# Order of turns, copies and projections in the fourth and the last four attention units

## The chip, the cores and the metric

The kernel runs on one core of a Trainium2 chip, as one launch. The metric is device time in microseconds (us); a run's time is that of the whole program on the core. The profiled execution has a span, from its first to its last instruction, and a time of its own, which is a little longer than the span.

## The reference

The input x has 32 batches of 100 tokens of width 512, the context has 722 tokens per batch. The reference computes x + attention(layernorm(x), context) and then x + feed-forward(layernorm(x)). The attention has 16 heads of width 32; its mask is lower triangular over 100 queries and 722 keys, so only the first 100 context tokens of a batch ever count:

```python
q = (Q @ WQ.T).reshape(B, Sq, NHEAD, D_K).transpose(0, 2, 1, 3)
k = (K @ WK.T).reshape(B, Skv, NHEAD, D_K).transpose(0, 2, 1, 3)
v = (V @ WV.T).reshape(B, Skv, NHEAD, D_K).transpose(0, 2, 1, 3)
scores = jnp.einsum('bhqd,bhkd->bhqk', q, k) / jnp.sqrt(jnp.float32(D_K))
causal = jnp.tril(jnp.ones((Sq, Skv), dtype=bool))
attn = jax.nn.softmax(jnp.where(causal, scores, -jnp.inf), axis=-1)
y = jnp.einsum('bhqk,bhkd->bhqd', attn, v).transpose(0, 2, 1, 3).reshape(B, Sq, D_MODEL)
return y @ Wfc.T + bfc
```

The feed-forward part has a shared expert for all 3200 tokens and 16 experts; each expert takes the 12 tokens of each batch with the highest routing score, and each is gelu(x Wg) * (x Wu) times Wd. All is float32.

## The kernel before

**Arithmetic.** A float32 matmul is made of three products: both operands are split into a rounded high part and the low remainder (a cast on ScalarE, a subtraction on VectorE or GpSimd), and high*high, high*low and low*high are added in PSUM (`mm3`, line 49, matmuls at line 56).

**Units.** Attention runs over 32 units. Unit u is block sb = u // 4 (four batches, 400 tokens) and column group c = u % 4 (four heads, 128 columns). `cur` holds the tiles by unit. The steps of a unit, each a small function:

- `kload(u)` (SyncE DMA of k from DRAM, tile kt), `qproj(u)` and `qkeep(u)`: q into PSUM (pool `a_kv`, two buffers) and its copy on ScalarE;
- `scores(u)`: 16 matmuls into the one buffer of tile sc;
- `sm_max(u, hb)` on VectorE, `sm_sub(u, hb)` on GpSimd, `sm_exp(u, hb)` on ScalarE, `sm_sum(u, hb)` on VectorE and `sm_mul(u, hb)` on GpSimd: softmax in two halves, hb = 0 and 1;
- `p_turn(u, b)`, `turns`: transposes of the probabilities of batch b of the block (0 to 3) into PSUM tile ms (pool `a_ms`, two buffers); `p_keep(u, b)`, `keeps`: the copies to tile pt on ScalarE. With two buffers the turns of batches 2 and 3 wait for the copies of 0 and 1, and `values` for the copy of 2;
- `values(u)`: attention times v into an ms tile; `y_keep(u)`: split of the result and its store to DRAM (yD).

The units overlap: the loop's pass u does q of unit u, the softmax of unit u - 1 and the turns and values of unit u - 2. The loop also projects k and v for later blocks: `kproj` (into a_kv), `kkeep` (copy kk on ScalarE and a store kD on SyncE), `vproj`, `vkeep`, and `vload(sb)`, which loads a block's v (tile v, 100 partitions, 800 KB) for its four units. Passes with no v left to project put `scores(u)` at their end (`ahead`).

**The order.** It is written out by hand: under `manual_schedule` TensorE, ScalarE, VectorE, SyncE and GpSimd each work their instructions strictly in program order. Who is ready later holds up what stands behind it on the same engine, and the DMAs of SyncE are issued in that order too.

**The last four units.** Pass 28 (`u == NU - 4`) is the last of the loop. Passes 29, 30 and 31 stand in `last_units(pr)`, where work of the feed-forward part is mixed in. `pr` prepares the first 384 tokens (three row tiles of 128): `pr.load_y()` loads attention output (yh, yl) back from yD, right after the loop and so ahead of pass 29 on SyncE; `pr.fc(i)` multiplies row tile i by Wfc into a_kv; `pr.add`, `pr.bias`, `pr.stats`, `pr.rsqrt`, `pr.norm` make the residual and the layer norm; `pr.turn(i)` transposes the row tile on TensorE and splits it (xh on ScalarE, xl on VectorE). `F.chunk_load`, `F.chunk_cast` and `F.chunk_low` bring and split the first weights of the feed-forward part. `F.preps[1]` is the same preparation for the next group of tokens. From `F.begin` on (gate_up of chunk 0) the feed-forward matmuls run.

Of the kernel before, what the change touches and what calls it, by code (L numbers as in the profile page):

```python
# [60 lines left out]
def attention(tc, K, F):  # L61
    nc = tc.nc
    with ExitStack() as ctx, ExitStack() as kvctx:
# [57 lines left out]
        def split_wc(w, c, r, eng=None):  # L121
            cs = slice(c * 128, (c + 1) * 128)
            split(WH[w][:, :, cs], WL[w][:, :, cs], r.rearrange("p (d n) -> p d n", d=NC4), eng)
# [122 lines left out]
        def qproj(u):  # L246
            sb, c = divmod(u, NC4)
            cs = slice(c * 128, (c + 1) * 128)
            nh, nl = cur["xh", sb], cur["xl", sb]
            pq = ps_kv.tile([128, D], F32, name="kv")  # L250
            mm3(nc, pq[:, 0:SB], [((WH[2][:, d, cs], WL[2][:, d, cs]),
                                   (nh[:, d, :], nl[:, d, :])) for d in range(NC4)])
            return pq

        def qkeep(u, pq):
            q = qp.tile([128, SB], F32, name="q")
            nc.scalar.copy(q, pq[:, 0:SB])
            cur["q", u] = q

        def scores(u):  # L260
            q, kt = cur["q", u], cur["k", u]
            sc = ps_sc.tile([S, 4, D], F32, name="sc")
            for b in range(4):
                cs = slice(b * S, (b + 1) * S)
                for h in range(4):
                    rows = slice(32 * h, 32 * h + 32)
                    nc.tensor.matmul(sc[:, h, cs], q[rows, cs], kt[rows, cs], start=True, stop=True)  # L267
            cur["sc", u] = sc
# [20 lines left out]
        def sm_exp(u, hb):  # L289
            p = cur["p", u, hb][0]  # L290
            for bb in range(2):
                b = u // NC4 * 4 + hb * 2 + bb
                nc.scalar.activation(p[:, bb], p[:, bb], AF.Exp, scale=rstd[:, b:b + 1])  # L293
# [8 lines left out]
        def sm_mul(u, hb):  # L302
            pv, sm = cur["p", u, hb][1], cur["sm", u, hb]
            nc.gpsimd.tensor_tensor(pv, pv, sm[:, :, None].to_broadcast([S, 8, S]), ALU.mult)  # L304
# [8 lines left out]
        def p_keep(u, b):  # L313
            pt = ptp.tile([128, 4, S], F32, name="pt")[0:S]
            nc.scalar.copy(pt, cur["tp", u, b][0:S, :, 0:S])  # L315
            cur["pt", u, b] = pt
# [20 lines left out]
        NU = nsb * NC4  # L337
# [78 lines left out]
        def turns(u, *bs):  # L416
            for b in bs:
                p_turn(u, b)

        def keeps(u, *bs):  # L420
            for b in bs:
                p_keep(u, b)
# [8 lines left out]
        def last_units(pr):  # L431

            gp, mt = nc.gpsimd, pr.pt

            def kt_bank():
                return ps_kv.tile([128, D], F32, name="kv").rearrange("p (c t) -> p c t", c=NC4)

            def maxes(u):
                for hb in range(2):
                    sm_max(u, hb)  # L440
                    sm_sub(u, hb)

            u = NU - 3
            kload(u)
            for i in range(pr.nt):
                pr.load_x(i)
            kload(u + 1)
            sm_max(u - 1, 0)
            sm_sub(u - 1, 0)
            y_keep(u - 3)  # L450
            sm_max(u - 1, 1)
            sm_sub(u - 1, 1)
            qkeep(u, qproj(u))
            turns(u - 2, 0, 1)
            keeps(u - 2, 0, 1)
            turns(u - 2, 2, 3)
            sm_exp(u - 1, 0)
            keeps(u - 2, 2, 3)
            sm_exp(u - 1, 1)
            for hb in range(2):  # L460
                sm_sum(u - 1, hb)
                sm_mul(u - 1, hb)
            pr.fc(0)
            F.chunk_load()
            values(u - 2)

            u = NU - 2
            scores(u - 1)
            y_keep(u - 3)
            pr.add(0)  # L470
            pr.bias(0)
            maxes(u - 1)
            pr.bias(1)
            pr.stats(0)
            pr.rsqrt(0)
            qkeep(u, qproj(u))
            turns(u - 2, 0, 1)
            keeps(u - 2, 0, 1)
            sm_exp(u - 1, 0)
            sm_exp(u - 1, 1)  # L480
            pr.fc(1)
            pr.norm(0)
            for hb in range(2):
                sm_sum(u - 1, hb)
                sm_mul(u - 1, hb)
            turns(u - 2, 2, 3)
            keeps(u - 2, 2, 3)
            pr.add(1)
            kload(u + 1)
            F.chunk_load()  # L490
            pr.store(0)
            pr.bias(2)
            values(u - 2)

            u = NU - 1
            scores(u - 1)
            y_keep(u - 3)
            maxes(u - 1)
            pr.fc(2)
            pr.add(2)  # L500
            pr.stats(1)
            pr.rsqrt(1)
            pr.stats(2)
            pr.rsqrt(2)
            F.ask(1, lambda: ps_kv.tile([128, D], F32, name="kv"))
            F.preps[1].load_x(0)
            F.preps[1].load_x(1)
            turns(u - 2, 0, 1)
            keeps(u - 2, 0, 1)
            qkeep(u, qproj(u))  # L510
            pr.pt = kt_bank
            pr.turn(0)
            pr.pt = mt
            pr.norm(1)
            pr.store(1)
            turns(u - 2, 2, 3)
            keeps(u - 2, 2, 3)
            pr.norm(2)
            pr.store(2)
            sm_exp(u - 1, 0)  # L520
            values(u - 2)
            sm_sum(u - 1, 0)
            sm_mul(u - 1, 0)
            y_keep(u - 2)
            pr.turn(1)
            sm_exp(u - 1, 1)
            sm_sum(u - 1, 1)
            sm_mul(u - 1, 1)
            F.chunk_cast(0, 0)

            scores(u)
            F.chunk_low(0, 0, gp)
            F.preps[1].fc(0)
            maxes(u)
            turns(u - 1, 0, 1)
            keeps(u - 1, 0, 1)
            turns(u - 1, 2, 3)
            keeps(u - 1, 2, 3)
            F.preps[1].fc(1)
            F.chunk_cast(0, 1)  # L540
            sm_exp(u, 0)
            sm_sum(u, 0)
            sm_mul(u, 0)
            pr.turn(2)
            sm_exp(u, 1)
            F.chunk_low(0, 1, gp)
            values(u - 1)
            sm_sum(u, 1)
            sm_mul(u, 1)
            y_keep(u - 1)  # L550
            F.chunk_cast(0, 2)
            scctx.close()
            F.open_gu()
            F.begin(pr.done())
            F.chunk_low(0, 2, gp)
            F.preps[1].add(0)
            F.preps[1].add(1)
            for i in range(3):
                F.chunk_cast(1, i)
                F.chunk_low(1, i, gp)  # L560
            F.preps[1].bias(0)
            F.preps[1].bias(1)
            turns(u, 0, 1)
            keeps(u, 0, 1)
            pr.logits()
            turns(u, 2, 3)
            keeps(u, 2, 3)
            F.begun()
            values(u)
            pr.tokens()  # L570
            y_keep(u)

        with tc.manual_schedule(engines={mybir.EngineType.Pool}):
            wq = prologue()
            ahead = False
            for u in range(NU - 3):
                sb, c = divmod(u, NC4)
                a, back = u - 1, u - 2
                a = a if a >= 0 else None
                back = back if back >= 0 else None  # L580
# [50 lines left out]
                if u == 1:  # L631
# [1 line left out]
                    wq_keep(2, wq[2])  # L633
                    sm_sum(a, 0)
                    sm_mul(a, 0)
                if a is not None and u > 2:
                    sm_exp(a, 0)
                if back is not None:
                    p_turn(back, 0)
                    p_turn(back, 1)  # L640
                    p_keep(back, 0)
                    p_keep(back, 1)
                if u == 2:
                    p_turn(back, 2)
                    p_turn(back, 3)
                    p_keep(back, 2)
                    p_keep(back, 3)
                    split_wc(2, 3, wq[3])
                    xt_split(1, 0)
                    sm_exp(a, 0)  # L650
                if xn:
                    x_stats(*xn)
                    if xn[1] == 3:
                        x_rstd(xn[0])
                if a is not None and u > 1:
                    sm_exp(a, 1)
                    sm_sum(a, 0)
                    sm_mul(a, 0)
                pk = kproj(j, ck) if kv else None
                if kv and vv:  # L660
                    kkeep(j, ck, pk)
                if u == 1:
# [2 lines left out]
                    sm_mul(a, 1)  # L665
                if c == 1 and u > 1 or u == NU - 4:
                    vload(sb)
                if back is not None and u > 2:
                    p_turn(back, 2)
                    p_turn(back, 3)  # L670
                    p_keep(back, 2)
                    p_keep(back, 3)
                if u == 1:
                    vkeep(j, ck, vproj(j, ck))
                    wq_less(3, wq[3])
                if kv and not vv:
                    kkeep(j, ck, pk)
                if a is not None and u > 1:
                    sm_sum(a, 1)
# [733 lines left out]
```

## Time and profile before

| | us |
|---|---|
| median of 3 runs | 1656.32 |
| lowest and highest run | 1654.76, 1657.05 |
| the profiled execution's own time | 1656.77 |
| its span | 1655.0 |
| TensorE (PE) busy in it | 1642.3 |
| VectorE (DVE) busy | 913.1 |
| ScalarE (ACT) busy | 697.4 |
| GpSimd (POOL) busy | 623.9 |

The page gives the time at which each engine was busy and the chain of waits that ended last. In the timelines a row is: start in us, length in us, engine, line, operation, output<-inputs, shape, count; in brackets the idle time of the engine just before the row, and what ended it. PEld is TensorE's loading of weights. SPq is SyncE's queue: a row there is the issue of a DMA, not its transfer. Attention lies in the first 360 us of the span (pass 3 starts near 55 us, pass 28 near 303, pass 31 near 330), and the feed-forward part fills the rest.

### The profile page before, as it was taken

The numbers are of one execution on the slowest core, as the hardware profiler recorded it, in microseconds if no ns is written. First come the engines' busy times: TensorE is split into PE (matmuls) and PEld (weight loads), VectorE is DVE, ScalarE is ACT, GpSimd is POOL, SyncE is SP. The second block draws the span as 40 slices with busy tenths as digits, with TensorE's granted clock in tenths as the row PEclk, the third lists the DMA queues.
The fourth block names the chain that finished last, engine by engine and source line by source line (L and its number), as shares of the span: only waits on it lengthen the run. The fifth ranks groups of instructions, "written<-read, shape, count | busy, mean of one in ns | idle before, by whom it ended". The sixth has DMA issues, their size and how long they took to land.

```text
span 1655.0 us, 27948 instructions
## 1 busy us (share of the span) xinstructions
PE 1642.3 (99%) x10722; PEld 1506.0 (91%) x10722; DVE 913.1 (55%) x2178; ACT 697.4 (42%) x1152; POOL 623.9 (38%) x501
## 2 busy tenths in 40 slices
PE   9999999999999999999999999999999999999999
PEld 8888888889899998999999999999999999999998
DVE  6878777665433434344655555555555555555542
ACT  4666666553111211123444444444444444444442
POOL 2778777660111011010743334433344443344001
PEclk9999999999999999999999999999999999999999
DMA  8566665645231223211545555455555455555452
GB/s 258 169 198 200 202 195 173 211 153 185 90 108 49 88 88 111 81 62 30 191 161 159 150 164 170 144 162 150 159 169 161 148 152 161 162 163 160 138 160 62
DMA packets 113493, 243.81 MB, mean 147 GB/s; under 512 B 16609, under 2 KB 64834, under 8 KB 113360
## 3 DMA queue, kind: packets, MB, share of 16 engines
q1 hardware_dynamic: 99856, 216.34, 39.8%
q0 software_dynamic: 13088, 25.22, 8.0%
q8 instruction: 84, 1.38, 0.3%
q14 instruction: 49, 0.40, 0.1%
q10 hardware_dynamic: 416, 0.48, 0.1%
HBM read 188.25 MB, written 53.73 MB: 146 GB/s over the span
## 4 chain that ended last, share of the span: by engine, by line
PE 95%; DVE 1%; POOL 1%; DMA 1%; ACT 1%; issue 1%; SPq 0%; POOLq 0%; ACTq 0%
PE gu L56 49%; PE dn L56 25%; PE kv L56 11%; PE m L56 3%; PE ms L310 2%; PE ms L325 1%; PE sc L267 1%; POOL p L287 1%; DMA yD<-y 0%; DVE p L278 0%; DMA yh<-yD 0%; PE m L1194 0%; DMA raw<-wA 0%; ACT pt L315 0%; POOL p L304 0%
## 5 line engine op out<-in xcount | busy, mean ns | idle before, releaser
L56 PE MATMUL gu<-xh,whl 128*128 128x384 f32 (+1 forms) x3200 | 641.2, 332 | 0.0
L56 PEld LDWEIGHTS gu<-xh,whl 128*128 128x128 f32 x3200 | 555.8, 188 | 20.3 <-issue 1.2
L1018 POOL DMA_INDIRECT gx<-xnD,iq x192 | 245.2, 1277 | 395.6 <-DVE big L1061 296.3
L56 PE MATMUL dn<-whl,hh 128*128 128x512 f32 x1168 | 366.3, 395 | 0.0
L821 DVE TENSOR_TENSOR whl<-wraw,whl 128x1536 fp32r<-128x1536 f32 x142 | 249.7, 1759 | 197.8 <-ACT whl L820 178.6
L56 PE MATMUL gu<-xl,whl 128*128 128x384 f32 (+1 forms) x1600 | 335.9, 331 | 0.0
L56 PEld LDWEIGHTS gu<-xl,whl 128*128 128x128 f32 x1600 | 279.1, 188 | 0.2 <-DVE xl L1052 0.2
L855 ACT CAST hh<-g 128x384 fp32r<-128x384 f32 (+1 forms) x200 | 101.0, 505 | 409.8 <-DVE g L852 379.2
L56 PEld LDWEIGHTS dn<-whl,hh 128*128 128x128 f32 x1168 | 215.7, 188 | 35.7
L852 DVE TENSOR_TENSOR g<-g,gu 128x384 f32<-128x384 f32 (+1 forms) x200 | 108.3, 541 | 251.0 <-PE gu L56 245.1
L820 ACT CAST whl<-wraw 128x1536 fp32r<-128x1536 f32 x142 | 209.8, 1477 | 57.2 <-PE dn L56 53.4
L56 PE MATMUL dn<-whl,hl 128*128 128x512 f32 x584 | 230.5, 395 | 0.0
L851 ACT ACTIVATE g<-gu 128x384 f32<-128x384 f32 (+1 forms) x200 | 96.2, 481 | 229.4 <-PE gu L56 229.4
L856 DVE TENSOR_TENSOR hl<-g,hh 128x384 fp32r<-128x384 f32 (+1 forms) x200 | 111.8, 559 | 114.3 <-ACT hh L855 113.8
L1073 POOL DMA_INDIRECT out_dram<-x,isl x48 | 77.7, 1619 | 171.0 <-ACT x L1072 161.2
L56 PEld LDWEIGHTS dn<-whl,hl 128*128 128x128 f32 x584 | 109.5, 188 | 26.1
L287 POOL TENSOR_TENSOR p<-p,mx 100x800 f32<-100x800 f32 x64 | 103.7, 1636 | 35.9 <-DVE mx L278 33.3
L304 POOL TENSOR_TENSOR p<-p,sm 100x800 f32<-100x800 f32 x64 | 97.4, 1528 | 35.6 <-DVE sm L299 26.2
L278 DVE CUSTOM_DVE_ANT_0 p<-sc,mask 100x100 f32<-100x100 f32 x512 | 95.5, 255 | 0.5 <-PE sc L267 0.5
L1110 POOL TENSOR_TENSOR x<-x,bfc 128x512 f32<-128x512 f32 x23 | 30.4, 1345 | 155.6 <-DMA x<-x 154.0
L293 ACT ACTIVATE p<-p,rstd 100x400 f32<-100x400 f32 x128 | 73.6, 624 | 17.6 <-POOL p L287 16.9
L1062 ACT CAST xh<-big 128x512 fp32r<-128x512 f32 x59 | 36.6, 621 | 101.4 <-DVE big L1061 101.4
(158 smaller groups left out, 1581.2 us busy)
## 6 DMA issues: line engine op xcount, KB each, us to landing
wraw<-wE SPq DMA_DIRECT2D x144, 768.0 KB
yD<-y SPq DMA_DIRECT2D x31, 400.0 KB
xr<-xT SPq DMA_DIRECT2D x32, 200.0 KB
vD<-vt SPq DMA_DIRECT2D x25, 256.0 KB
v<-vD SPq DMA_DIRECT2D x8, 800.0 KB
xnD<-xn SPq DMA_DIRECT2D x25, 256.0 KB
out_dram<-x SPq DMA_DIRECT2D x25, 256.0 KB
kt<-kD SPq DMA_DIRECT2D x31, 200.0 KB
```

The lines of the kernel that those rows point to most:

```text
L56: r = nc.tensor.matmul(out, t[0][a], t[1][b], start=(first and i == 0), stop=(last and i == n - 1))
L278: nc.vector.tensor_tensor_reduce(out=p[:, bb, h, :], in0=sc[:, h, cs], in1=mask, scale=ISCALE, scalar=NEG, op0=ALU.add, op1=ALU.max, accum ...
L287: nc.gpsimd.tensor_tensor(pv, pv, mx[:, :, None].to_broadcast([S, 8, S]), ALU.subtract)
L304: nc.gpsimd.tensor_tensor(pv, pv, sm[:, :, None].to_broadcast([S, 8, S]), ALU.mult)
L820: nc.scalar.copy(h, r)
L821: nc.vector.tensor_tensor(l, r, f32(h), ALU.subtract)
L851: nc.scalar.activation(g[:, 0:t], pg[:, 0:t], AF.Gelu)
L852: nc.vector.tensor_tensor(g[:, 0:t], g[:, 0:t], pu[:, 0:t], ALU.mult)
L855: nc.scalar.copy(hh[:, 0:t], g[:, 0:t])
L856: nc.vector.tensor_tensor(hl[:, 0:t], g[:, 0:t], f32(hh[:, 0:t]), ALU.subtract)
L1018: nc.gpsimd.indirect_dma_start(out=g[:, k, :], out_offset=None, in_=self.K.xn.rearrange("t (a f) -> (t a) f", f=128), in_offset=bass.Indir ...
L1073: ins = nc.gpsimd.indirect_dma_start(out=self.K.out, out_offset=bass.IndirectOffsetOnAxis(ap=r.isl[:, i:i + 1], axis=0), in_=o, in_offset= ...
```

## The change

The change moves calls; it adds and removes none, and every instruction keeps its operands.

- Pass 3: the turns and copies of batches 2 and 3 go right behind those of 0 and 1, ahead of the exponentials and of `kproj`, as pass 2 already had them (`early`).
- Pass 28: `kproj` is called ahead of the turns of batches 2 and 3 (as TensorE had it already); the copies of batches 2 and 3 and `kkeep`, with its DMA, go ahead of the second half's exponential, and so ahead of `vload`.
- Pass 29: `pr.fc(0)` and the first half's exponential go between the two pairs of turns.
- Pass 30: the turns and copies of batches 2 and 3 go ahead of the second half's exponential and of `pr.norm(0)`, behind `pr.fc(1)`.
- Pass 31: the turns and copies of batches 2 and 3 go ahead of `pr.turn(0)`; `scores(u)` and the second half's exponential, sum and product go ahead of `pr.turn(1)`.

```diff
--- before.py
+++ after.py
@@ -453,14 +453,14 @@
             qkeep(u, qproj(u))
             turns(u - 2, 0, 1)
             keeps(u - 2, 0, 1)
+            pr.fc(0)
+            sm_exp(u - 1, 0)
             turns(u - 2, 2, 3)
-            sm_exp(u - 1, 0)
             keeps(u - 2, 2, 3)
             sm_exp(u - 1, 1)
             for hb in range(2):
                 sm_sum(u - 1, hb)
                 sm_mul(u - 1, hb)
-            pr.fc(0)
             F.chunk_load()
             values(u - 2)
 
@@ -477,14 +477,14 @@
             turns(u - 2, 0, 1)
             keeps(u - 2, 0, 1)
             sm_exp(u - 1, 0)
+            pr.fc(1)
+            turns(u - 2, 2, 3)
+            keeps(u - 2, 2, 3)
             sm_exp(u - 1, 1)
-            pr.fc(1)
             pr.norm(0)
             for hb in range(2):
                 sm_sum(u - 1, hb)
                 sm_mul(u - 1, hb)
-            turns(u - 2, 2, 3)
-            keeps(u - 2, 2, 3)
             pr.add(1)
             kload(u + 1)
             F.chunk_load()
@@ -508,13 +508,13 @@
             turns(u - 2, 0, 1)
             keeps(u - 2, 0, 1)
             qkeep(u, qproj(u))
+            turns(u - 2, 2, 3)
+            keeps(u - 2, 2, 3)
             pr.pt = kt_bank
             pr.turn(0)
             pr.pt = mt
             pr.norm(1)
             pr.store(1)
-            turns(u - 2, 2, 3)
-            keeps(u - 2, 2, 3)
             pr.norm(2)
             pr.store(2)
             sm_exp(u - 1, 0)
@@ -522,13 +522,13 @@
             sm_sum(u - 1, 0)
             sm_mul(u - 1, 0)
             y_keep(u - 2)
-            pr.turn(1)
+            scores(u)
             sm_exp(u - 1, 1)
             sm_sum(u - 1, 1)
             sm_mul(u - 1, 1)
+            pr.turn(1)
             F.chunk_cast(0, 0)
 
-            scores(u)
             F.chunk_low(0, 0, gp)
             F.preps[1].fc(0)
             maxes(u)
@@ -633,30 +633,42 @@
                     wq_keep(2, wq[2])
                     sm_sum(a, 0)
                     sm_mul(a, 0)
-                if a is not None and u > 2:
+                if a is not None and u > 3:
                     sm_exp(a, 0)
                 if back is not None:
                     p_turn(back, 0)
                     p_turn(back, 1)
                     p_keep(back, 0)
                     p_keep(back, 1)
-                if u == 2:
+                early = u in (2, 3)
+                if early:
                     p_turn(back, 2)
                     p_turn(back, 3)
                     p_keep(back, 2)
                     p_keep(back, 3)
+                if u == 2:
                     split_wc(2, 3, wq[3])
                     xt_split(1, 0)
+                if early:
                     sm_exp(a, 0)
                 if xn:
                     x_stats(*xn)
                     if xn[1] == 3:
                         x_rstd(xn[0])
+                pk = None
+                if u == NU - 4:
+                    pk = kproj(j, ck)
+                    p_turn(back, 2)
+                    p_turn(back, 3)
+                    p_keep(back, 2)
+                    p_keep(back, 3)
+                    kkeep(j, ck, pk)
                 if a is not None and u > 1:
                     sm_exp(a, 1)
                     sm_sum(a, 0)
                     sm_mul(a, 0)
-                pk = kproj(j, ck) if kv else None
+                if kv and not pk:
+                    pk = kproj(j, ck)
                 if kv and vv:
                     kkeep(j, ck, pk)
                 if u == 1:
@@ -665,7 +677,7 @@
                     sm_mul(a, 1)
                 if c == 1 and u > 1 or u == NU - 4:
                     vload(sb)
-                if back is not None and u > 2:
+                if back is not None and not early and u < NU - 4:
                     p_turn(back, 2)
                     p_turn(back, 3)
                     p_keep(back, 2)
@@ -673,7 +685,7 @@
                 if u == 1:
                     vkeep(j, ck, vproj(j, ck))
                     wq_less(3, wq[3])
-                if kv and not vv:
+                if kv and not vv and u < NU - 4:
                     kkeep(j, ck, pk)
                 if a is not None and u > 1:
                     sm_sum(a, 1)
```

## The prediction

> **What bounds the kernel now.** I read the page first (shares, then the chain), then TensorE's waits by stretch, then the timelines of the engines and of SP's queue around the edited units, then DMA by stretch.
>
> ```profile
> PE 1642.3 (99%) x10722; PEld 1506.0 (91%) x10722; DVE 913.1 (55%) x2178; ACT 697.4 (42%) x1152; POOL 623.9 (38%) x501
> PE 95%; DVE 1%; POOL 1%; DMA 1%; ACT 1%; issue 1%; SPq 0%; POOLq 0%; ACTq 0%
> ```
>
> TensorE is busy 1642.3 of 1655.0 us and carries 95% of the chain. The edit removes no matmul, so it can only gain out of 12.7 us of TensorE idle, and any new TensorE wait is added whole. TensorE's waits in the window from 300 us (the last units lie at 303 to 360):
>
> ```profile
> PE ms L325 <- ACT pt L315: 1.5, 3, 0.8
> PE kv L56 <- DMA yh<-yD: 0.8, 1, 0.8
> PE ms L310 <- POOL p L304: 0.6, 1, 0.6
> PE ms L1050 <- DVE xn L1140: 0.5, 1, 0.5
> PE ms L310 <- ACT pt L315: 0.4, 1, 0.4
> ```
>
> With 0.2 for x L1119 that is 4.0 us; unit 3 has one more wait, 1.83 us at 63.23. So about 5.9 us is the most to be had. Where they sit in unit 29, TensorE's timeline:
>
> ```profile
> 313.52 0.85 PE L310 MATMUL ms<-ident,p 100*100 100x100 f32 x8
> 314.75 0.86 PE L310 MATMUL ms<-ident,p 100*100 100x100 f32 x8 [0.39 <-ACT pt L315]
> 316.43 1.19 PE L56 MATMUL kv<-wfh,yh 128*128 128x512 f32 x4 [0.81 <-DMA yh<-yD]
> 319.67 0.89 PE L325 MATMUL ms<-pt,v 100*32 100x100 f32 x32
> ```
>
> Turns, turns, fc(0), values. fc(0) starts the moment yh lands. SP's queue, which issues that load:
>
> ```profile
> 304.55 0.31 SPq L242 DMA_DIRECT2D v<-vD  x1
> 311.14 0.32 SPq L232 DMA_DIRECT2D kD<-kk  x1
> 311.52 0.43 SPq L1099 DMA_DIRECT2D yh<-yD  x1
> 312.04 0.53 SPq L1099 DMA_DIRECT2D yl<-yD  x1
> ```
>
> The reader is to see that v, 800 KB, goes out 6.6 us ahead of kD, which waits for the kk copy on ACT, and that yh follows kD at once. And DMA by stretch (last columns: DMA share, GB/s), while v alone moves and while yh and yl move:
>
> ```profile
> 308.00:310.00 2.00, 2.00 (x35) 1.67 (x37) 1.19 (x2) 2.00 (x6) 0.80 (x2) 1.00 0.62 199
> 316.00:317.00 1.00, 0.57 (x3) 0.49 (x4) 0.85 (x1) 1.00 (x4) 0.30 (x1) 1.00 1.05 396
> ```
>
> v has 100 partitions; its share is 0.62, 10 of 16 engines, and the landing records show ten reports for it against sixteen for yh.
>
> **Part 1, unit 3.** Copies (keeps) go ahead of the exponentials, turns 2,3 ahead of kproj. Now keeps 0,1 wait behind exp(2,0), which waits for POOL's subtraction until 61.5, and turns 2,3 start at 63.23 after 1.83 us idle. Unit 2 already has the new order: turns at 47.50, turns 2,3 at 48.73 (0.38 idle), kproj at 49.37. So turns 58.40, kproj 60.27, vproj 62.5 instead of 63.87: TensorE is 1.4 us ahead. But the softmax chain isn't. exp(2,1) still waits for POOL until 63.03 and ends at 64.2 instead of 64.5; the two keeps behind it (0.89) leave, so the sum on DVE starts at 64.3 instead of 64.99; then two xnl splits (2.39) and y (0.56), and unit 3's maxima start at about 68.3 instead of 68.93, POOL's subtraction at 69.9 instead of 70.60. In unit 4 the next turns 2,3 (73.83 now) wait for keeps behind exp(3,0), which waits for that subtraction. That wait is late next and gives back half: kept 0.7 us (bounds 0.3 and 1.4).
>
> **Part 2, unit 28.** TensorE's order is unchanged. On ACT keeps 2,3 and kk go ahead of exp(27,1): a copy starts 0.6 us after its turns (345.84 to 346.48), so keep 2 at 309.27, kk ends 310.53 instead of 311.12. exp(27,1) moves from 308.81 to 310.45, its sum by 1.65 us; cover: its product is needed only by turns 27, 2,3, which come after fc(0).
>
> What the diff doesn't say is on SP: kkeep issues a DMA, and moves ahead of vload. The order becomes kD, v, yh, yl, kt, x. v therefore waits behind kD's wait for kk and goes out at 310.93 instead of 304.55, 0.4 us ahead of yh. What that costs: earlier v loads have the same order kD, v and other DMAs behind. Issued at 279.48, v's ten engines report from 285.62 to 286.59; issued at 240.49, 247.36 to 248.40; over all eight the last comes 7.1 to 9.4 us after the issue. The vD store issued at 281.60 reports last at 286.96, 0.37 us after v's last: on the engines that v uses, what is behind it waits. Each of them then has a sixteenth of yh to move, 2.1 us (yh reported 315.58 to 316.38, yl 317.70 to 318.50). So v ends at 310.93 + 7.65 = 318.6 (bounds 318.0 and 320.3) and yh at 320.7 (bounds 320.1 and 322.4; below that 316.2, if v and yh did not share engines at all). yl follows 2.1 us later, as fc(0) needs it; kt, due at scores(29), then at about 324, is just in time; v itself is needed only by values(28).
>
> **Part 3, unit 29.** fc(0) goes between turns 0,1 and turns 2,3; keeps 2,3 ahead of exp(28,1). TensorE ends turns 0,1 at about 314.3 and then stands before fc(0) until 320.7: 6.4 us idle instead of 1.2. fc(0) is 4.3 us later (320.7 less 316.43). Turns 2,3, which now covered part of the wait, come behind: 3.05 for fc(0), turns at 323.8, keep 2 from 324.4 to 324.85, values at 324.95 instead of 319.67, +5.3. Queued on ACT behind keeps 2,3 is exp(28,1), now done at 317.9, then at 326.35; DVE waits with its sum, y, add(0), and maxima(29) start at 328.7 instead of 322.24.
>
> **Parts 4 and 5, units 30 and 31.** In 30, keeps 2,3 ahead of exp(29,1) would save about 0.4 of the 0.8 us before values, but keep 2 now waits for exp(29,0), behind the late maxima: values(28) at 333.7, +4.9. In 31, turns 2,3 go ahead of pr.turn(0), scores ahead of pr.turn(1), the second sum ahead of xl(1). The late DVE and POOL chain (+6.3) sets pr.turn(0) at 343.05, xn(1) and so pr.turn(1) at 346.3, fc at 346.9 (+5.4), mul(30,0) and turns(30,0,1) at 350.0 (+5.6). The second sum one split earlier gives its product 0.6 back: turns(30,2,3) at 351.5, and gate_up(0) at 356.44 instead of 350.79: +5.65, that is fc(0)'s 4.3 and 1.35. Chunk casts and lows shift by the same. Nothing behind this recovers it: from there TensorE runs without a wait.
>
> Sum so far: 5.65 - 0.7 = +5.0 us.
>
> **The clock.** The start of the trace shows TensorE at half pace: 128x256 matmuls begin 0.215 us apart until 14.04, then 0.12.
>
> ```profile
> 13.61 0.41 PE L56 MATMUL kv<-cxh,wh 128*128 128x256 f32 x1
> 13.83 0.41 PE L56 MATMUL kv<-cxl,wh 128*128 128x256 f32 x1
> 14.20 0.28 PE L56 MATMUL kv<-cxh,wh 128*128 128x256 f32 x1
> 14.32 0.29 PE L56 MATMUL kv<-cxl,wh 128*128 128x256 f32 x1
> ```
>
> (The granted clock shows 1.00 there too, so the pace is what to read.) After 14 us no idle of TensorE is over 1.83 us and the pace never falls, so by the trace alone a stall costs its length: +5.0. The Trainium skill, "TensorE: Matmul & The Clock Gate", section "What's actually happening", says that a free-running window of about 3.4 us without work sets the array back to half clock, and that a busy window brings full clock back. It speaks against this change: 6.4 us hold a whole window in (6.4 - 3.4)/3.4, nearly 9 executions in 10. Half pace then lasts from fc(0) to the end of the first busy window, 3.4 to 6.8 us, and costs half of that, 1.7 to 3.4. My estimate from that page is 2.5 (bounds 0, and about 4 if the short wait before values spoils a window). With it the sum is +7.5. I take it, since the start of this trace shows that such a state exists and needs a dense stretch to end.
>
> Against the profiled execution's own time of 1656.77 (1.77 around its span): 1664.3. That execution lies 0.45 over the median of the runs, 1656.32, so I forecast a median of 1663.8.
>
> **Rivals.** (a) Stall without a clock drop: +5.0, 1661.3. For it: nothing in the trace shows a drop in mid-kernel; against: the rule and the length of the gap. (b) v is not in yh's way, because engines share out both loads or v goes faster than any of the eight: yh at 316.2, fc(0) 0.2 earlier than now, and -0.2 + 1.35 - 0.7 = +0.4, 1656.8: not slower. It decides at yh landing before 319.0, where 2.6 + 1.35 - 0.7 makes 3.3 us. Against it stand the eight v loads and the vD report. (c) The reordering does what it says: yh is there when TensorE comes at 314.3, the waits of unit 29 go, 1.2 us less 0.5 for values' new wait, half of the 2.5 us in 30 and 31 goes, and 0.7 to 1.4 in unit 3: -2.6 to -3.3, about 1653.4. It needs yh 2 us earlier than now with more queued ahead of it.
>
> **How the numbers follow.** Full case 0.55 (1661.8 to 1667), (a) 0.25 (1659.9 to 1663), (b) 0.15, (c) 0.05. The range 1658.5 to 1667.0 leaves out most of (b) and (c) and a little at the top. 0.2% is 3.3 us, about what a measurement of this kernel can tell from no change. Slower by more than that: the full case and nearly all of (a), 0.80; within: 0.15; faster: 0.05.
>
> **What would show it.** Right: SP issues kD, v, yh within 1 us near 310 us; TensorE's longest wait is fc(0) on yh, 5 to 7 us; its matmuls of 128x512 behind it start about 0.43 apart instead of 0.23; unit 3's 1.83 shrinks to 0.4 with a new wait of about 0.7 in unit 4; gate_up(0) near 358. Wrong: yh landing within 7 us of kD's issue, or TensorE's wait at fc(0) under 3 us, would throw the sum over; full pace after a gap over 5 us would leave +5.0.

## The result and the profile after

The changed kernel takes 1663.82 us in the median of five runs (1663.54 to 1664.44), the kernel before 1656.32 (1654.76 to 1659.09 in five). The ratio is 1.0043 with a 95% interval of 1.0031 to 1.0054: slower by 0.4%, clear of zero. The profiled execution has a span of 1661.8 us.

The page, the rows for the engines and the chain:

```profile
PE 1642.1 (99%) x10722; PEld 1504.5 (91%) x10722; DVE 913.0 (55%) x2178; ACT 697.4 (42%) x1152; POOL 624.8 (38%) x501
PE 93%; DVE 2%; DMA 1%; POOL 1%; ACT 1%; issue 1%; SPq 0%; POOLq 0%; ACTq 0%; DVEq 0%
```

TensorE is busy for as long as before; what was added is TensorE's idle time. Five rows of its waits over the whole span name it (engine, line, waited for: total us, times, longest):

```profile
PE kv L56 <- DMA yh<-yD: 5.3, 1, 5.3
PE ms L310 <- ACT pt L315: 2.8, 5, 1.3
PE ms L310 <- POOL p L304: 1.4, 3, 0.6
PE ms L310 <- DVE y L105: 0.9, 1, 0.9
PE kv L56 <- DVE xnl L105: 0.6, 1, 0.6
```

One wait for yh of 5.3 us stands where 0.8 us stood. SyncE's queue shows why:

```profile
309.51 0.32 SPq L232 DMA_DIRECT2D kD<-kk  x1
309.92 0.32 SPq L242 DMA_DIRECT2D v<-vD  x1
310.30 0.49 SPq L1111 DMA_DIRECT2D yh<-yD  x1
310.88 0.46 SPq L1111 DMA_DIRECT2D yl<-yD  x1
```

kD, v and yh go out within 0.8 us. In the landing records v's ten engines report from 316.78 to 317.62. Of yh's sixteen reports six come from 317.12 to 317.55 and ten from 318.93 to 319.50. TensorE's timeline in unit 29 and at the start of unit 30:

```profile
312.42 0.51 PE L310 MATMUL ms<-ident,p 100*100 100x100 f32 x4
313.81 0.55 PE L310 MATMUL ms<-ident,p 100*100 100x100 f32 x4 [0.89 <-DVE y L105]
319.64 2.04 PE L56 MATMUL kv<-wfh,yh 128*128 128x512 f32 x4 [5.28 <-DMA yh<-yD]
321.48 1.91 PE L56 MATMUL kv<-wfl,yh 128*128 128x512 f32 x4
323.19 1.36 PE L56 MATMUL kv<-wfh,yl 128*128 128x512 f32 x4
324.38 0.85 PE L310 MATMUL ms<-ident,p 100*100 100x100 f32 x8
325.53 0.89 PE L325 MATMUL ms<-pt,v 100*32 100x100 f32 x32 [0.29 <-ACT pt L315]
330.17 1.17 PE L56 MATMUL kv<-wfh,yh 128*128 128x512 f32 x4
```

The reader is to see two things: fc(0) starts as yh lands, and its groups of four take 2.04 and 1.91 us where the same groups of fc(1) at 330.17 take 1.17: half pace. The trace's clock record has 0.50 from 316.91 for 6.83 us, to 323.74; before it had no such stretch in mid-kernel. (That record begins at 14.13 in the kernel before, where the pace doubles; ahead of it there is no entry, and the 1.00 that the prediction read there is no reading of the clock.)

ACT holds the second effect, the exponentials queued behind the two copies. The second half's exponential of unit 28, before and then in the changed kernel, where the copies ahead of it waited 8.76 us for the turns:

```profile
316.69 1.17 ACT L293 ACTIVATE p<-p,rstd 100x400 f32<-100x400 f32 x2
```

```profile
324.98 0.89 ACT L315 COPY pt<-ms 100x400 f32<-100x400 f32 x2 [8.76 <-PE ms L310]
325.75 1.16 ACT L293 ACTIVATE p<-p,rstd 100x400 f32<-100x400 f32 x2
```

To compare executions I cut each trace at the same TensorE starts: unit 3's qproj, unit 5's qproj, unit 28's qproj, fc(0), unit 30's qproj, the first gate_up. Steps in us:

| trace | unit 3 to 5 | 28 to gate_up | of it 29 to fc(0) | fc(0) to 30 | 30 to gate_up |
|---|---|---|---|---|---|
| before | 20.26 | 47.29 | 5.21 | 4.95 | 29.41 |
| changed | 20.90 | 55.09 | 9.52 | 7.60 | 30.29 |
| v first | 20.88 | 48.53 | 4.70 | 5.91 | 30.24 |
| v late alone | 21.73 | 55.05 | 10.60 | 7.32 | 29.42 |
| filled gap | 21.03 | 53.58 | 9.60 | 6.01 | 30.29 |
| part 1 alone | 20.90 | 47.16 | 5.10 | 4.95 | 29.39 |
| parts 4, 5 alone | 22.66 | 46.51 | 5.05 | 4.95 | 28.79 |
| yh first, parts 4, 5 | 22.31 | 45.36 | 4.17 | 4.69 | 28.78 |
| part 1, early split | 20.89 | 47.47 | 5.39 | 4.98 | 29.38 |
| parts 3, 4, 5 | 20.56 | 51.02 | 5.72 | 7.30 | 30.28 |
| yh first, parts 1, 4, 5 | 20.90 | 45.39 | 4.17 | 4.70 | 28.79 |
| yh first again | 22.52 | 45.39 | 4.18 | 4.69 | 28.80 |

Between the two profiled executions the spans differ by 6.8: 0.64 in units 3 to 5, 7.80 from unit 28 to gate_up, 0.23 in between and 0.04 behind, less 1.93 that arose before unit 3, where the edit changes nothing: TensorE's full clock came at 14.13 us in the execution before and at 6.30 in the one after. This start differs from run to run (4.1 to 14.1 us over the traces), so the steps are read, not the spans.

### The profile page after: what moved, and what is told of

Read it like the earlier page. It is cut to its first block, busy times and chain, and to the rows that moved or that the text cites. A ratio compares the mean times of both kernels' runs of the same rounds, so it can differ in the third digit from the quotient of the medians.

```text
span 1661.8 us, 27950 instructions
## 1 busy us (share of the span) xinstructions
PE 1642.1 (99%) x10722; PEld 1504.5 (91%) x10722; DVE 913.0 (55%) x2178; ACT 697.4 (42%) x1152; POOL 624.8 (38%) x501
## 4 chain that ended last, share of the span: by engine, by line
PE 93%; DVE 2%; DMA 1%; POOL 1%; ACT 1%; issue 1%; SPq 0%; POOLq 0%; ACTq 0%; DVEq 0%
PE gu L56 49%; PE dn L56 25%; PE kv L56 10%; PE m L56 3%; PE ms L310 2%; PE sc L267 1%; PE ms L325 1%; POOL p L287 1%; DMA raw<-wA 1%; DMA yh<-yD 1%; DVE p L278 0%; DVE sm L298 0%; DVE xnl L105 0%; POOL p L304 0%; ACT p L293 0%
## 5 line engine op out<-in xcount | busy, mean ns | idle before, releaser
L56 PEld LDWEIGHTS gu<-xh,whl 128*128 128x128 f32 x3200 | 555.8, 188 | 20.3 <-issue 1.7
L298 DVE TENSOR_REDUCE sm<-p 100x8 f32<-100x800 f32 x64 | 62.8, 982 | 33.7 <-ACT p L293 32.4
```

The source lines that it names most:

```text
L56: r = nc.tensor.matmul(out, t[0][a], t[1][b], start=(first and i == 0), stop=(last and i == n - 1))
```

## The experiments

The times below stand against runs of the kernel before on the same chip.

**v first again.** The changed kernel with v's load put back ahead of kD. Theory A: v's late issue is the cause. Theory B: the new order of turns, copies and exponentials is.

```diff
                     p_keep(back, 3)
+                    vload(sb)
                     kkeep(j, ck, pk)
...
-                if c == 1 and u > 1 or u == NU - 4:
+                if c == 1 and u > 1:
                     vload(sb)
```

> The changed kernel with one thing undone: in pass 28 vload goes ahead of kkeep again, so v is issued near 304 us and kD and yh come behind it as before. If v's late issue holds up yh (theory A), yh lands near 316 again, fc(0) waits under 2 us instead of 5.3, the clock does not drop, and what remains against before is fc(0) ahead of turns 2,3 (+1.35 by the prediction's sum) and unit 3 (+0.6 by the changed kernel's trace): about 1658 us. If the new order of turns, copies and exponentials costs by itself (theory B), the time stays at 1662 or more and fc(0)'s wait at 4 us or more.

Measured: 1658.66 us against 1657.18, ratio 1.0009 (1.0002 to 1.0016). TensorE's timeline:

```profile
316.37 1.17 PE L56 MATMUL kv<-wfh,yh 128*128 128x512 f32 x4 [0.47 <-DMA yh<-yD]
317.37 1.10 PE L56 MATMUL kv<-wfl,yh 128*128 128x512 f32 x4
```

yh landed at 316.23, the wait is 0.47, the pace is full, and unit 28 to gate_up is 48.53: 6.56 of the 7.80 us are gone with one call moved back. What stays is 1.24.

**v late, alone.** The same move made in the kernel before, and nothing else.

```diff
-                if c == 1 and u > 1 or u == NU - 4:
+                if c == 1 and u > 1:
                     vload(sb)
...
                     kkeep(j, ck, pk)
+                if u == NU - 4:
+                    vload(sb)
```

> The kernel before with one thing changed: in pass 28 vload goes behind kkeep. Everything else stands as before. Theory A: v is issued 0.4 us ahead of yh, yh lands near 320.5 instead of 316.4, TensorE waits about 5.2 us at fc(0) instead of 0.8; +4.2 us, and +2 more where the clock drops (a 5.2 us gap holds a whole window of 3.4 us in about half of the executions): 1660.5 to 1663 us. Theory B: one late load of v moves nothing, within 0.5 us of before.

Measured: 1663.15 us against 1657.18, ratio 1.0035 (1.0025 to 1.0044).

```profile
315.12 0.87 PE L310 MATMUL ms<-ident,p 100*100 100x100 f32 x8 [0.39 <-ACT pt L315]
322.19 2.07 PE L56 MATMUL kv<-wfh,yh 128*128 128x512 f32 x4 [6.20 <-DMA yh<-yD]
324.06 1.91 PE L56 MATMUL kv<-wfl,yh 128*128 128x512 f32 x4
```

yh landed at 322.15, v at 320.23, 8.3 us after its issue. With turns 2,3 still ahead of fc(0) the step 28 to gate_up is 55.05, +7.76: the late load alone makes as much as the whole change. That the two sums are so near is chance: part 3 gives nothing here, but fc(0) comes 5.39 us later against unit 29 instead of 4.31, and the clock was at half for 10.24 us (317.81 to 328.05), longer than I had allowed. Theory A holds, B falls for all but 1.2 us.

**Filled gap.** What does the clock cost?

```diff
+            fill = ps_kv.tile([128, D], F32, name="kv")
+            for _ in range(18):
+                nc.tensor.matmul(fill, F.wfh[:, 0, 0:128], F.wfh[:, 0, :], start=True, stop=True)
+            pr.pm = lambda: fill
             pr.fc(0)
+            pr.pm = lambda: ps_kv.tile([128, D], F32, name="kv")
```

> The changed kernel with 18 extra matmuls of 128x512 on the resident weights wfh ahead of fc(0), into the PSUM tile that fc(0) then overwrites; they add no result. 18 x 0.23 = 4.1 us lie inside the gap of 5.3 us. If the half-clock stretch costs about 2 us (clock part of theory A), TensorE stays at full clock, fc(0) takes 2.9 to 3.1 us instead of 4.7, and the time falls by about 2.0, to 1661.8 us. If only the wait counts (rival a of the prediction), nothing changes: 1663.8 us.

Measured: 1662.55 us against 1657.18, ratio 1.0030 (1.0017 to 1.0043).

```profile
314.53 4.34 PE L458 MATMUL kv<-wfh 128*128 128x512 f32 x18
320.11 1.19 PE L56 MATMUL kv<-wfh,yh 128*128 128x512 f32 x4 [1.24 <-DMA yh<-yD]
321.13 1.10 PE L56 MATMUL kv<-wfl,yh 128*128 128x512 f32 x4
```

yh lands as late as ever (29 to fc(0) 9.60 against 9.52), but fc(0) runs at full pace: fc(0) to unit 30 is 6.01 instead of 7.60. The half-clock stretch costs 1.6 us in this step; the late fc(0) and the late chain are as they were. The medians differ by 1.3 (1662.55 and 1663.82), but they come from two sets of runs; it is the step that shows the cost.

**Part 1 alone** (`early = u in (2, 3)` in the kernel before).

> The kernel before with part 1 alone (unit 3: copies ahead of exponentials, turns 2,3 ahead of kproj). The prediction's step says 0.7 us gained by the start of unit 5. The changed kernel's trace, measured from unit 3's turns (56.48) to unit 5's qproj (75.09), gives 18.61 against 17.98 before (58.40 to 76.38), so 0.6 us lost, with new waits of 0.6 on xnl and 1.3 on the copies. Theory A1 (xnl splits on DVE lie behind GpSimd's products): 18.6 again, and two xnl splits in 3.3 us instead of 2.4. Rival (the loss comes from elsewhere in the changed kernel): 17.3. In the whole time either is under 1 us and hardly to be told.

Measured: 1657.38 against 1657.18, ratio 0.9997 (0.9988 to 1.0007); unit 3 to 5 20.90, as theory A1 had it. The changed kernel shows where it goes. xnl is the low part of the split x that qproj multiplies, and the maxima of the unit stand behind its two splits on VectorE. VectorE before:

```profile
64.99 0.99 DVE L298 TENSOR_REDUCE sm<-p 100x8 f32<-100x800 f32 x1 [0.96 <-ACT kk L226]
66.13 2.39 DVE L105 TENSOR_TENSOR xnl<-xr,xnh 128x400 fp32r<-128x400 f32 x2
```

VectorE, then TensorE, in the changed kernel:

```profile
62.78 0.98 DVE L298 TENSOR_REDUCE sm<-p 100x8 f32<-100x800 f32 x1 [0.66 <-ACT kk L226]
63.92 3.32 DVE L105 TENSOR_TENSOR xnl<-xr,xnh 128x400 fp32r<-128x400 f32 x2
67.16 0.56 DVE L105 TENSOR_TENSOR y<-ms,y 128x400 fp32r<-128x400 f32 x1
```

```profile
67.29 0.45 PE L56 MATMUL kv<-xnl,wh 128*128 128x400 f32 x1 [0.63 <-DVE xnl L105]
72.54 0.87 PE L310 MATMUL ms<-ident,p 100*100 100x100 f32 x8 [1.28 <-ACT pt L315]
```

The second split takes 2.87 us here, from 64.37 to 67.24; before it took 1.90, from 66.63 to 68.52. In both kernels GpSimd's second product and the ctx splits (of the context) follow each other without a gap. Before, the split of xnl ended 0.43 us behind the product (68.09); here it waited out the first ctx split too and ended 0.44 us behind that (66.80). TensorE waits for it 0.63 in unit 4. Against unit 3's qproj, the sum starts 0.28 earlier than before and the two splits take 0.93 longer, so the maxima start 0.64 later instead of 0.6 earlier, and so do the turns of batches 2 and 3 in unit 4, with a wait of 1.28.

**Part 1 with one split earlier**, to take it out of GpSimd's way.

```diff
+                if u == 3:
+                    xt_split(1, 2)
                 if early:
                     sm_exp(a, 0)
...
                 if u == 3:
-                    xt_split(1, 2)
                     xt_split(1, 3)
```

> Part 1 alone, with one of unit 3's two xt_split calls moved ahead of the exponentials, where ScalarE and VectorE wait for GpSimd. From unit 3's qproj to unit 5's: 20.26 us before, 20.90 with part 1. Theory A1 (part 1 loses because the two xnl splits run beside GpSimd's products, 3.3 us instead of 2.4, and hold up qproj of unit 4 and the maxima): the wait of 0.6 on xnl goes, the maxima of unit 3 start a microsecond earlier, 19.2 to 19.9 us. Rival (the copies behind the exponentials set it in any order): 20.5 to 21.

A miss: 20.89, and 1655.7 us against 1656.37, ratio 0.9997 (0.9988 to 1.0006). The splits met other work of GpSimd:

```profile
60.39 1.88 DVE L105 TENSOR_TENSOR xnl<-xr,xnh 128x400 fp32r<-128x400 f32 x1 [0.22 <-ACT xnh L104]
65.22 2.72 DVE L105 TENSOR_TENSOR xnl<-xr,xnh 128x400 fp32r<-128x400 f32 x1
```

The first ends 0.44 us behind GpSimd's subtractions (58.79 to 61.83), the second 0.43 us behind its products (64.50 to 67.51). The Trainium skill, "SBUF — State Buffer", section "SBUF: two separate sides", says that VectorE and GpSimd share a port pair that one of them holds for a whole instruction, and that a VectorE operation with two SBUF inputs needs it against a GpSimd operation that reads SBUF. The rows agree: xnl reads two SBUF tiles and takes 1.88 to 2.87 us where GpSimd was at work first, 0.56 to 0.58 without GpSimd; the y split, which reads one of its inputs from PSUM, takes 0.56 beside GpSimd's work too. This run doesn't decide between the theory and its rival: the rival's 20.5 to 21 came true, but the splits were no shorter. That they make part 1's loss is read from the timelines; no run frees them of GpSimd.

**Parts 4 and 5 alone.**

> The kernel before with parts 4 and 5 alone (units 30 and 31). Measured on the trace from unit 28's qproj to the first gate_up: before 47.29 us. The prediction's parts 4 and 5 hold that these edits would gain 0.4 in unit 30 and a part of the 1.7 us of waits in unit 31 if the softmax chain were not late: 46.1 to 46.7 us, the chain (VectorE and GpSimd) setting the rest. Rival: the chain sets unit 31 whatever TensorE's order is, 47.2 us.

Measured: 28 to gate_up 46.51, as expected, 0.78 less than before, 0.62 of it from unit 30 on. The whole time doesn't tell it: 1656.74 against 1656.37, ratio 1.0002 (0.9994 to 1.0010).

**Parts 3, 4 and 5**, without part 2's copies: where do the 1.24 us of the run with v first come from?

> The kernel before with parts 3, 4 and 5, without parts 1 and 2, so v is issued early as before. The run with v ahead of kkeep took 48.53 us from unit 28's qproj to gate_up, +1.24 against before. If this comes from part 3 (turns 2,3 and the second exponential behind fc(0)), it stays: 48.4 to 48.7 us, with the step from fc(0) to unit 30's qproj at 5.9 instead of 4.95. If it comes from part 2 (copies of unit 28 ahead of its second exponential), it goes: 46.1 to 47.3 us.

Measured: 1658.86 against 1656.37, ratio 1.0016 (1.0009 to 1.0022). The sum is a miss: 51.02, over both forecasts. The step 30 to gate_up is 30.28, as in the changed kernel, so the late chain belongs to part 3: the second exponential stands behind copies that stand behind fc(0). fc(0) to unit 30 took 7.30 here instead of the 5.9 expected; the clock had dropped again, after a wait of only 2.58 us. And 29 to fc(0) took 5.72, where the run with v first has 4.70: without part 2's early copies kD and yh are issued 0.5 us later against unit 29, which is half of it. TensorE:

```profile
316.49 2.00 PE L56 MATMUL kv<-wfh,yh 128*128 128x512 f32 x4 [2.58 <-DMA yh<-yD]
318.29 1.86 PE L56 MATMUL kv<-wfl,yh 128*128 128x512 f32 x4
319.99 1.10 PE L56 MATMUL kv<-wfh,yl 128*128 128x512 f32 x4
```

**yh first, with parts 4 and 5.** If what stands ahead of yh in SyncE's queue sets fc(0), the queue can be turned to advantage. v's load is taken out of pass 28, and there kkeep keeps kD's DMA back for `last_units`. What is issued there, behind yh and yl:

```diff
             u = NU - 3
+            nc.sync.dma_start(*cur.pop("kk"))
             kload(u)
...
             kload(u + 1)
+            vload(NU // NC4 - 1)
```

> The kernel before with parts 4 and 5, and with the DMAs of pass 28 in another order: the loads yh and yl first, then kD, kt, the rows of x, kt, and v last. If what is queued ahead of yh on SyncE is what sets fc(0) (theory A), yh lands before 312 us, fc(0) follows turns 2,3 without a wait, 0.8 us less than before: unit 28's qproj to gate_up in 45.3 to 45.9 us, v landing near 323, ahead of values(28) near 327. Rival: v or a kt comes too late instead and scores(29) or values(28) waits for it; then 47 us or more.

Measured: 1654.86 against 1656.37, ratio 0.9990 (0.9983 to 0.9996): faster by 0.1% than the kernel before, and so than the changed one. SyncE's queue, then TensorE:

```profile
304.97 0.37 SPq L1104 DMA_DIRECT2D yh<-yD  x1
311.58 0.33 SPq L447 DMA_DIRECT2D kD<-kk  x1
315.65 0.37 SPq L245 DMA_DIRECT2D v<-vD  x1
```

```profile
315.19 0.86 PE L313 MATMUL ms<-ident,p 100*100 100x100 f32 x8 [0.39 <-ACT pt L318]
315.83 1.17 PE L56 MATMUL kv<-wfh,yh 128*128 128x512 f32 x4
```

yh landed at 311.29 and fc(0) follows turns 2,3 without a wait; 28 to gate_up is 45.36, 1.93 under before and 1.15 under parts 4 and 5 alone. v landed at 324.90; no wait for it is seen.

**The same with part 1, and the same again.**

> The version with yh and yl first and parts 4 and 5, plus part 1. Two traces of kernels without part 1 show the clock at half pace for 3.4 us behind unit 3's wait of 1.8 to 2.0 us, and 21.7 to 22.7 us from unit 3's qproj to unit 5's instead of 20.3; traces with part 1 show 20.9 and no drop. Theory (part 1 costs 0.6 us where the clock holds and saves 1 to 2 where it drops): 20.9 us, no drop near 61 us, unit 28's qproj to gate_up again 45.4, and a median within 0.6 us of the version without part 1, with less scatter between runs. Rival (part 1 only loses): 0.6 us over that version's median of 1654.9.

> The version without part 1 once more, on the same chip as the one with it, for the comparison: 1654.9 us, and unit 3's qproj to unit 5's 20.3 us where the clock holds, 21.7 to 22.7 where it drops.

Measured: 1654.05 with part 1 and 1654.06 without, against 1655.92; ratios 0.9989 (0.9981 to 0.9997) and 0.9986 (0.9980 to 0.9993). The medians show neither a gain nor a loss of part 1. In the traces it is a trade, in the step from unit 3 to 5: 20.9 to 21.0 in all six with it and no clock drop there; without it 20.26 and 20.56 where the clock held, 21.73 to 22.66 in the four where it dropped. Less scatter between runs was expected and isn't shown: 1652.84 to 1656.79 and 1652.54 to 1656.88.

## Why the prediction was right, and where it was not

- **v behind kk on SyncE: right.** This step carries the result. fc(0) came 4.31 us later against unit 29 than before; 4.3 was forecast, and v and yh landed where the eight earlier v loads put them. Undoing it took 6.56 of 7.80 us away, making it alone gave 7.76.
- **Turns and exponential behind fc(0): right, undersized.** 1.35 was forecast; the run with v first has 0.96 from fc(0) to unit 30 and 0.83 behind it.
- **The clock: right that it drops, by the wrong rule, and oversized.** 2.5 was taken, the filled gap gives 1.6. The forecast needed a window wholly without work. In the profiled execution there was none: the turns at 313.81 lie in the window that ended with the drop (below), and fc(0) began in the next. By that rule the clock would have held there.
- **Parts 4 and 5: right.** Their gain was forecast to be mostly lost behind the late chain, and was; alone they gain 0.6 from unit 30 on.
- **Part 2's cover: right in effect, incomplete.** I named only the product as delayed. The later maxima also hold up the split of y(26), which holds an ms buffer: a new wait of 0.89 at 313.81. It lies inside the wait for yh and cost nothing here.
- **Part 1: wrong in sign.** -0.7 was forecast, +0.64 measured. The forecast had the maxima 0.6 earlier; they came 0.6 later. Two terms failed. The larger is "two xnl splits (2.39)": a duration read in one place was carried to another, where the second split waited out two of GpSimd's instructions instead of one, and it became 3.32. The smaller is the start of the sum, put at 64.3 right behind exp(2,1): on the same scale it came at 64.7, behind the kk copy, on which the sum waits in the kernel before too (0.96 in its row above). The wait in unit 4 was foreseen at 0.7 and was 1.28, and the 0.63 for xnl was not.
- **The sum.** From unit 28 on 4.31 + 1.79 + 1.6 makes 7.7 of the 7.8 measured, for 8.15 forecast; with unit 3 the steps give 8.4 for 7.5 forecast. That the median of 1663.8 was met to the decimal is luck: part 1's error, the oversized clock and the chance of the start partly cancel. The steps, not the hit, are the evidence. Rival (a) falls with the half pace of fc(0); (b) and (c) fall with yh's landing.

## What to carry to other kernels

A call that is moved takes its DMA along: read the issue order of each queue before and after, and ask what large load now stands ahead of what small deadline. A duration taken from one place in the trace holds in another only if what it ran beside there is the same; here it was GpSimd. On a TensorE that is otherwise always busy, a wait of about 2 us can cost more than its length: where it lay in one window, the clock was at half for the next, and the step from unit 3 to 5 took 21.7 to 22.7 us instead of 20.3. Filling or moving such a wait can be worth more than the wait.

## What the runs showed of the hardware

- **The clock drops on a half-idle window, not only on an idle one.** Windows are 3.413 us: half-clock stretches last 3.413, 6.827 and 10.240 us, and the full-clock stretch of the kernel before lasts 481 of them. With parts 4 and 5 alone, unit 3's wait of 2.03 us was enough:

```profile
62.51 1.43 PE L310 MATMUL ms<-ident,p 100*100 100x100 f32 x8 [2.03 <-ACT pt L315]
63.63 2.05 PE L56 MATMUL kv<-wh,cxh 128*128 128x512 f32 x4
65.49 1.36 PE L56 MATMUL kv<-wl,cxh 128*128 128x512 f32 x4
```

  TensorE's busy time (second column: us, and matmuls) in the window that ends with that drop, in the one of the run with v late alone, and in the window behind the same wait in the kernel before, where the clock held:

```profile
59.24:62.65 3.41, 1.38 (x10) 1.00 0.37 140
```

```profile
58.40:61.81 3.41, 1.57 (x11) 1.00 0.43 158
```

```profile
61.91:65.33 3.42, 2.10 (x14) 1.00 0.00 0
```

  So 46% busy drops it and 61% does not. The windows of all twelve traces, cut from the start of each full-clock stretch on, sort the same way: of 5780 windows at full clock, the 13 that were busy for 46% or less (seven of them in mid-kernel) were each followed by half clock, and none of the others was. The least busy of those has 56%, in the run with parts 4 and 5 alone, late in the kernel; here it is, and with it the window that ends with the drop in the changed kernel:

```profile
1649.85:1653.26 3.41, 1.90 (x9) 1.00 0.18 68
```

```profile
313.50:316.91 3.41, 0.55 (x4) 1.00 1.06 241
```

  Where the limit lies between 46% and 56% stays open, and so does whether the busy share counts or the longest gap in the window: that was 1.8 us or more in the 13, and 1.5 us or less in the others. The Trainium skill, "TensorE: Matmul & The Clock Gate", section "What's actually happening", speaks of an idle window; none of the 13 was wholly idle, so here the measurement decides. Whether a given wait of 1.8 us counts depends on where the window's edge falls in it. The way back asks for more: in the run with v late alone a window at half clock that was 72% busy (321.22 to 324.64) was followed by another at half clock, hence the 10.24 us.
- **A load over 100 partitions holds up what follows on its ten engines for the length of the load.** yh landed 9.2 us after its issue behind v in the changed kernel, and 4.9 us after it in the kernel before, where v was done. In the changed kernel ten of yh's sixteen reports came 1.9 us or less behind v's last and six came 1.4 to 2.4 us ahead of those ten; the run with v late alone has the same six (319.12 to 319.70) and ten (321.38 to 322.15). The six were late as well, 6.8 us or more after the issue instead of 4.1 to 4.9, though v has only ten reports. Why, no run shows.
